# Softmax maxima folded by DMAs through memory, and a division with five transposes in the side bank: one change to an attention and feed-forward kernel on one Trainium2 core

## The chip, the cores and the metric

The kernel runs on one core of one Trainium2 chip. The metric is the device time of one execution in microseconds (us). The engines are named as in the profile: PE is TensorE (PEld its weight loads), DVE is VectorE, ACT is ScalarE, POOL is GpSimd and SP is SyncE, which here issues most DMAs. An engine takes its instructions in order. SBUF is the on-chip memory; PSUM is the memory that PE writes, here eight banks of 128 partitions x 512 fp32.

## The reference

```python
x = x + layernorm(attention(layernorm(x)))          # x: 4 x 1024 x 256, fp32
x = x + layernorm(ffn(layernorm(x)))

# attention, 16 heads of 16
scores = q @ k.T / sqrt(16)
exp_x = exp(clip(scores - max(scores), -50, 50))
attn = exp_x / (sum(exp_x) + 1e-6)
y = (attn @ v) @ Wout.T
# ffn, ternary weights with a scale for each output; hidden size 1024
h = silu(x @ w1.T * s1) * (x @ w2.T * s2)
h = gelu(h @ h1.T * sh1); h = gelu(h @ h2.T * sh2)
y = h @ w3.T * s3
```

The kernel takes the exponential without subtracting the maximum. The sum of the exponentials then has to get eps times the exponential of the maximum in place of eps, so a maximum of each row is wanted once, in the division at the end. (The program takes the maximum over keys only for the first 128 queries of each half; for the others it tests a bound on the scores, and a general version stands behind a branch.)

## The kernel before

**Attention stage.** The work is cut into 32 units: 4 batches (b) x 4 groups of 4 heads (g) x 2 halves of 512 queries (h). Units are numbered 0 to 31 in that order, so an even number is a first half (h = 0) and an odd one a second half. A unit has 16 tiles: 8 chunks of 128 keys x 2 pairs of heads. For a tile, `exponentials` (L444) makes two score products on PE (L451, `s`), into one two-bank PSUM buffer of the pool `ps` (tag "big", three buffers), and one exponential of 128x1024 on ACT (L452, `e`) into a ring of eight tiles in SBUF. For each chunk, `weigh` (L454) multiplies the exponentials of four heads with the values (L459, `acc`, one PSUM bank; the profile shows a chunk as x8); a row of ones among the values gives the sum. For each chunk but the first, `rise` (L461) takes the running maximum over chunks on DVE (L468, `top`, 128 keys x 4 heads x 128 queries).

**Turns.** The order is written out by the loop at L937. A turn makes three tiles (`TURN`), issues the maxima of tiles that earlier turns made, weighs the chunks that are ready (one or two, `a` or `aa` below), and then takes one step of side work that uses PE, with such steps as use no PE. The side work (`Side`, L551) is a list of chains of steps; a step has a gap, the number of turns that it keeps from the step before it in its chain. Chains in `first` go before the others. It holds the next batch's layer norm, transposes (L301), projections (`p`), values (`pv`) and checks (`pn`, `pr`), the output projection of the batch that ends (L506, `py`), and the division of each unit. All but the division use the one PSUM bank `misc` (the side bank). The eighth bank is `acc`.

**A unit's end** (`unit_end`, L632): DVE moves `acc` to SBUF (L265, `o`), and the division (`divide`, L470) is queued as a step with a gap of 1, that is for the side work of the same turn. It takes one of the three "big" buffers: four transposes of `top` into one bank (L478), four of `o` into the other (L480); DVE takes the maximum over the 128 keys from PSUM (L482, `em`), adds eps times it to the sums (L485), copies the others (L486), inverts (L487) and multiplies into `on` (L488). While it holds that buffer, `side.borrowed` makes the next turn begin with two tiles, with the third after its weighing (L940, L959).

**SP's queue.** At the end of a second half, `stack` (L419) issues 32 copies of 64 KB from SBUF to SBUF (L413), which lay out the q and k of the group after the next. Their target is free when the last score product of the unit that just ended has read it. Near the end of the stage SP also issues the loads of the feed-forward weights (L683): twelve after unit 27, four after unit 29.

**Feed-forward stage** (from about 645 us): 8 halves of 512 rows, PE nearly always busy. `prepare` (L707) normalises the next half and transposes it into the side bank (L728), as steps of side work.

Of the kernel before, what the change touches and what calls it, by code (L numbers as in the profile page):

```python
# [25 lines left out]
ROWS = PARTS * DH  # L26
RING = 8
TURN = 3
LN_EPS = 1e-5
# [86 lines left out]
def tile_fast(ctx: ExitStack, tc: tile.TileContext, x, wqk, wv, wo, w1, w1s, w2, w2s, h1, h1s, h2, h2s, w3, w3s, out, bad):  # L116
# [12 lines left out]
    small = ctx.enter_context(tc.tile_pool(name="small", bufs=3))  # L129
    dram = ctx.enter_context(tc.tile_pool(name="rounded", bufs=1, space=bass.MemoryType.DRAM))  # L130


# [45 lines left out]
    with ExitStack() as actx, ExitStack() as rctx:  # L178
# [88 lines left out]
        def prologue(b, space, copy):  # L267
# [61 lines left out]
            def squares(w, m, h):  # L329
                def run():  # L330
                    sq = st["sq", w, m] = work.tile([P, NQ], BF16, tag="sq", name="sq", bufs=4)
                    hi = cq[w, m, "hi"][:, h * NQ : (h + 1) * NQ].bitcast(F32)
                    nc.scalar.activation(sq, hi, AF.Square)

                return run
# [125 lines left out]
        def rise(k):  # L461
# [4 lines left out]
            if c:  # L466
                top = tops[b, g, h]
                nc.vector.tensor_max(top, top if c > 1 else pair(k - 2)[:, :, :, 0:P], pair(k)[:, :, :, 0:P])  # L468

        def divide(g, h, o, top):  # L470


            def run():
                side.borrowed = True
                both = ps.tile([P, 2, NQ], F32, tag="big", name="po")
                po, pm = both[:, 0], both[:, 1].rearrange("p (i k) -> p i k", k=P)
                for i in range(HPG):
                    nc.tensor.transpose(pm[:, i], top[:, i // 2, i % 2], ident)  # L478
                for t in range(TPQ):
                    nc.tensor.transpose(po[:, t * P : (t + 1) * P], o[:, t * P : (t + 1) * P], ident)  # L480
                em = small.tile([P, HPG], F32, tag="em", name="em")
                nc.vector.tensor_reduce(em, pm, AX.X, ALU.max)  # L482
                po = po.rearrange("p (t i s) -> p t i s", t=TPQ, s=SLOT)
                den = small.tile([P, TPQ, HPG], F32, tag="den", name="den")
                nc.vector.scalar_tensor_tensor(den[:, 0], em, SM_EPS, po[:, 0, :, DH], ALU.mult, ALU.add)  # L485
                nc.vector.tensor_copy(den[:, 1:], po[:, 1:, :, DH])  # L486
                nc.vector.reciprocal(den, den)  # L487
                nc.vector.tensor_mul(  # L488
                    on[h][:, :, HPG * DH * g : HPG * DH * (g + 1)].rearrange("p t (i e) -> p t i e", e=DH),
                    po[:, :, :, 0:DH], den.unsqueeze(3).to_broadcast([P, TPQ, HPG, DH]),  # L490
                )

            return [Step(run, 1)]
# [57 lines left out]
        class Side:  # L551


            def __init__(self):
                self.first, self.rest, self.slot = [], [], 0
                self.tired = False
                self.borrowed = False

# [23 lines left out]
            def take(self, calm=False):  # L582

                self.slot += 1
                self.borrowed = False
                free, heavy = True, False
                for chain in self.first + self.rest:
                    while (step := self.due(chain, self.slot, free)) and (step.tensor or not calm):
                        chain[0].pop(0)
                        chain[1] = self.slot  # L590
                        step.run()
                        free = free and not step.tensor
                        heavy = heavy or step.heavy
                self.tired = heavy
# [6 lines left out]
        accs, tops, ends, later = {}, {}, {}, {"qk1": None}  # L601

        def begin(b):

            if b + 1 < B:
                norm, xt, qk, v, flags = prologue(b + 1, misc, to_vector)

                def first_made():
                    later["qk"] = b + 1
                    side.add(flags[0])  # L610

                def second_made():
                    later["qk1"] = b + 1
                    side.add(flags[1])

# [16 lines left out]
        def unit_end(b, g, h):  # L632
# [4 lines left out]
            assert g or not b or not any(step.tensor for step in ends[b - 1, h][0])  # L637
            unit = side.add(divide(g, h, o, tops[b, g, h]), True)
            if g == NG - 1:
# [13 lines left out]
            if at < B:  # L653
                put = Step(slots(at, n), 0, False)
                if at > b:
                    assert later["qk"] == at
                    later["chain"][0].append(put)
                else:
                    assert later["qk1"] == at
                    put.run()  # L660
                stack(at, n)
            if g == NG - 3 and b + 1 < B:
# [44 lines left out]
        def prepare(n, copy):  # L707
# [26 lines left out]

            return norm_steps(rows, st) + [Step(apply(i), 1, False) for i in range(0, TPQ, 2)] + [Step(transposes(c), 1) for c in range(DC)]

# [187 lines left out]
        early = [v[1], Step(slots(0, 0, 0, NT // 2), 0, False)]  # L924
        side.add(early + v[2:] + [Step(slots(0, 0), 0, False), Step(slots(0, 1), 0, False)] + sum(qk[1], []) + [Step(lambda: later.update(qk1=0, v=0), 0, False), Step(lambda: side.add(flags[0] + flags[1]), 0, False)])
        begin(0)
# [10 lines left out]
        while weighed < len(tiles):  # L937
            n = end = made
            end += TURN
            make(end - side.borrowed)  # L940
            if made == len(tiles):
# [262 lines left out]
```

## Time and profile before

| | us |
|---|---|
| median of 3 runs (1323.52 to 1325.0) | 1324.16 |
| the profiled execution, its own time | 1322.63 |
| its span | 1320.8 |
| attention stage, about | 17 to 645 |
| PE busy, share of the span | 1267.2 (96%) |
| ACT busy | 724.1 (55%) |
| DVE busy | 696.2 (53%) |
| POOL busy | 119.1 (9%) |

The shares are means over two stages with different limits: ACT is busy 83 to 89% of each 100 us between 100 and 600 us, and 186 of the 670 us from 650 us on. PE's busy time holds matmuls whose ends are modelled, and matmuls on different rows or columns of the array overlap. In a group's line, the first number after the bar is the busy time, the second the mean duration in ns, and after the second bar stands the engine's idle time just before these instructions, with what ended it.

### The profile page before, as it was taken

What the parts mean: (1) busy time and instruction counts of PE and PEld (TensorE: products, weight loads), DVE (VectorE), ACT (ScalarE), POOL (GpSimd) and SP (SyncE); (2) the same over time, 40 slices, a digit from 0 to 9 for tenths busy, and PEclk for the clock granted to TensorE, in tenths of its full rate; (3) what the DMA queues carried; (4) which work ended last, traced back from release to release, by engine and by line L of the source; (5) the groups of instructions that cost most, each with busy time, mean ns of one, the idle gap of its engine ahead of it and who ended that gap; (6) DMA issues with size and microseconds to landing.
All of it is one profiled execution on the core that took longest, in us unless ns stands there. A gap on an engine that the chain in (4) does not pass through costs nothing.

```text
span 1320.8 us, 21125 instructions
## 1 busy us (share of the span) xinstructions
PE 1267.2 (96%) x8194; PEld 777.2 (59%) x8194; DVE 696.2 (53%) x1518; ACT 724.1 (55%) x902; POOL 119.1 (9%) x166
## 2 busy tenths in 40 slices
PE   7999999999999999988999999999999999999995
PEld 3333333333333333333578888788887888878885
DVE  3456457654685445645662634736446364463533
ACT  4788887888888888898631412314223142231410
POOL 6212112121120000000000000000000000000000
PEclk9999999999999999999999999999999999999998
DMA  4685543466443333343220000201101011020000
GB/s 131 171 212 131 118 114 94 110 143 152 73 114 61 50 50 65 65 95 129 80 113 1 24 1 1 64 25 32 56 1 64 24 33 57 1 64 8 17 0 19
DMA packets 45518, 91.30 MB, mean 69 GB/s; under 512 B 12000, under 2 KB 22880, under 8 KB 45408
## 3 DMA queue, kind: packets, MB, share of 16 engines
q1 hardware_dynamic: 37520, 65.20, 21.4%
q0 software_dynamic: 7360, 24.12, 5.8%
q8 instruction: 67, 1.10, 0.4%
q10 hardware_dynamic: 528, 0.52, 0.1%
q14 instruction: 43, 0.35, 0.1%
HBM read 40.52 MB, written 15.73 MB: 43 GB/s over the span
## 4 chain that ended last, share of the span: by engine, by line
PE 76%; DVE 10%; ACT 9%; issue 3%; POOL 1%; DMA 1%; SPq 0%; ACTq 0%; POOLq 0%; DVEq 0%
PE ph L739 35%; PE acc L459 12%; PE s L451 8%; ACT e L452 7%; PE pg L739 5%; PE pz L792 4%; PE p L259 4%; PE py L259 2%; PE pv L259 2%; DVE top L468 2%; PE po L480 1%; DVE sg L755 1%; DVE o L265 1%; DVE st L94 1%; DVE ha_lo L744 1%
## 5 line engine op out<-in xcount | busy, mean ns | idle before, releaser
L452 ACT ACTIVATE e<-s 128x1024 f32<-128x1024 f32 x512 | 485.1, 1034 | 54.5 <-PE s L451 42.9
L459 PE MATMUL acc<-e,vaug 128*32 128x512 f32 x2048 | 255.1, 600 | 2.6 <-POOL vaug L429 2.6
L775 ACT ACTIVATE a<-ph,h_scale 128x512 f32<-128x512 f32 x128 | 81.1, 686 | 306.6 <-PE ph L739 306.6
L451 PE MATMUL s<-sq,sk 64*128 64x512 f32 x1024 | 193.2, 449 | 17.6 <-ACT e L452 15.0
L739 PE MATMUL ph<-hb_hi,h 128*128 128x512 f32 x512 | 199.5, 390 | 0.0
L739 PE MATMUL ph<-hb_lo,h 128*128 128x512 f32 x512 | 199.4, 389 | 0.0
L451 PEld LDWEIGHTS s<-sq,sk 64*128 64x128 f32 x1024 | 86.2, 184 | 158.3 <-ACT e L452 125.8
L468 DVE TENSOR_TENSOR top<-top,e 128x512 f32<-128x512 f32 x192 | 134.6, 701 | 42.0 <-ACT e L452 35.4
L459 PEld LDWEIGHTS acc<-e,vaug 128*32 128x32 f32 x2048 | 49.2, 108 | 107.2 <-issue 97.6
L104 POOL TENSOR_TENSOR rstd<-ve,minus_half 128x4 f32<-128x4 f32 (+1 forms) x33 | 37.5, 1137 | 803.1 <-DVE ve L102 803.1
L739 PEld LDWEIGHTS ph<-hb_hi,h 128*128 128x128 f32 x512 | 96.1, 188 | 20.2
L739 PEld LDWEIGHTS ph<-hb_lo,h 128*128 128x128 f32 x512 | 96.1, 188 | 20.1
L776 DVE CAST ha_hi<-a 128x512 fp32r<-128x512 f32 x64 | 27.1, 424 | 142.5 <-ACT a L775 142.5
L739 PE MATMUL ph<-ha_hi,sq 128*128 128x512 f32 x256 | 101.8, 398 | 0.3
L739 PE MATMUL ph<-ha_lo,sq 128*128 128x512 f32 x256 | 99.9, 390 | 0.0
L739 PE MATMUL ph<-ha_lo,sk 128*128 128x512 f32 x256 | 99.7, 390 | 0.0
L739 PE MATMUL ph<-ha_hi,sk 128*128 128x512 f32 x256 | 99.7, 390 | 0.0
L753 ACT ACTIVATE sg<-pg,w_scale 128x512 f32<-128x512 f32 x64 | 43.3, 688 | 55.0 <-DVE ha_lo L744 43.1
L755 DVE SCALAR_TENSOR_TENSOR sg<-pg,w_scale,sg 128x512 f32<-128x512 f32 x64 | 47.1, 745 | 48.0 <-ACT sg L753 48.0
L776 DVE CAST hb_hi<-a 128x512 fp32r<-128x512 f32 x64 | 27.0, 422 | 71.3 <-ACT a L775 71.3
L259 PE MATMUL p<-xT,wqk_sb 128*32 128x512 f32 x512 | 61.1, 598 | 1.5 <-ACT xT L262 0.9
L739 PEld LDWEIGHTS ph<-ha_hi,sq 128*128 128x128 f32 x256 | 48.4, 189 | 12.7 <-DVE sg L755 3.3
(158 smaller groups left out, 1648.2 us busy)
## 6 DMA issues: line engine op xcount, KB each, us to landing
w<-in_h_dram POOLq DMA_DIRECT2D x16, 512.0 KB, 5.5
h_r<-wr POOLq DMA_DIRECT2D x16, 512.0 KB, 3.8
x<-in_h_dram SPq DMA_DIRECT2D x32, 256.0 KB, 2.7
sk<-ck1hi SPq DMA_DIRECT2D x64, 64.0 KB, 2.3
sk<-ck1lo SPq DMA_DIRECT2D x64, 64.0 KB, 2.3
sq<-cq1hi SPq DMA_DIRECT2D x64, 64.0 KB, 2.3
sq<-cq1lo SPq DMA_DIRECT2D x64, 64.0 KB, 2.3
h<-h_r SPq DMA_DIRECT2D x8, 512.0 KB, 6.5
```

The source lines that it names most:

```text
L104: nc.gpsimd.tensor_tensor(rstd[:, :n], ve[:, :n], self.minus_half[:, :n], ALU.pow)
L259: nc.tensor.matmul(o[j : j + SLOT, :], w[:, j : j + SLOT], i, **flags)
L451: nc.tensor.matmul(s[:, a, :], stacks[1, g % 2, u][r, c * P : (c + 1) * P], stacks[0, g % 2, u][r, h * NQ : (h + 1) * NQ], start=True, sto ...
L452: nc.scalar.activation(pair(k)[:, u], s, AF.Exp)
L459: nc.tensor.matmul(acc[SLOT * i : SLOT * (i + 1), :], vaug[g % 2][:, c, i, :], pair(k)[:, i // 2, i % 2, :], start=c == 0, stop=c == NT - 1)
L468: nc.vector.tensor_max(top, top if c > 1 else pair(k - 2)[:, :, :, 0:P], pair(k)[:, :, :, 0:P])
L739: nc.tensor.matmul(p, homes[n][c][:, m * P : (m + 1) * P], half[:, c, :], start=c == 0 and k == 0, stop=c == len(homes[n]) - 1 and k == 1)
L753: nc.scalar.activation(sg, p[:, 0, :], AF.Silu, scale=scales["w1"][:, m : m + 1])
L755: nc.vector.scalar_tensor_tensor(sg, p[:, 1, :], scales["w2"][:, m : m + 1], sg, ALU.mult, ALU.mult)
L775: nc.scalar.activation(a, p[:, j, :], AF.Gelu, scale=scales[n][:, m : m + 1])
L776: nc.vector.tensor_copy(o[0][:, m, :], a)
L792: nc.tensor.matmul(p[t], half[:, c, t * P : (t + 1) * P], homes["w3"][c], start=c == 0 and k == 0, stop=c == HC - 1 and k == 1)
```

## The change

The division of 30 of the 32 units is split into transfers, a fold and a shorter division.

- At a unit's end, `divide` at once issues five DMAs on SP: `top` is spilled to a buffer in device memory (256 KB), and for each of the four heads it is read back (64 KB) into `folded`, so that 32 partitions hold one head, and four keys of it lie side by side. Reading back waits for the spill to land; the spill waits for the last maximum. These DMAs stand in SP's queue ahead of the stack copies of the same `unit_end`.
- A step `fold` (no PE; gap 4 in first halves, 3 in second halves) takes two maxima on DVE, over 128x256 and 128x128, which leaves 32 partial maxima for each head.
- A step `run` (gap 1 behind the fold) does four transposes of `o` and one of `folded` into the side bank. The fifth writes into columns of `o`'s slots that are not otherwise used (`HOLE`). DVE's reduction reads 128x(4x32) from there. What follows is as before.
- No turn is shortened: `side.borrowed` is gone.
- The last two units keep the old division (`divide_last`).
- Small moves: the two chains of checks (`flags`) become one; the stack copies may be issued later where the second half of q and k isn't ready (`pending`); the buffer `sq` has two copies instead of four; in `prepare` the first transpose keeps a gap of 2 instead of 1.

```diff
+    shuffle = ctx.enter_context(tc.tile_pool(name="shuffle", bufs=2, space=bass.MemoryType.DRAM))
...
-                    sq = st["sq", w, m] = work.tile([P, NQ], BF16, tag="sq", name="sq", bufs=4)
+                    sq = st["sq", w, m] = work.tile([P, NQ], BF16, tag="sq", name="sq", bufs=2)
...
+        def quotients(g, h, em, po):
+            den = small.tile([P, TPQ, HPG], F32, tag="den", name="den")
+            nc.vector.scalar_tensor_tensor(den[:, 0], em, SM_EPS, po[:, 0, :, DH], ALU.mult, ALU.add)
+            nc.vector.tensor_copy(den[:, 1:], po[:, 1:, :, DH])
+            nc.vector.reciprocal(den, den)
+            nc.vector.tensor_mul(
+                on[h][:, :, HPG * DH * g : HPG * DH * (g + 1)].rearrange("p t (i e) -> p t i e", e=DH),
+                po[:, :, :, 0:DH], den.unsqueeze(3).to_broadcast([P, TPQ, HPG, DH]),
+            )
+
         def divide(g, h, o, top):
+            there = shuffle.tile([P, HPG, P], F32, tag="top", name="top_d")
+            nc.sync.dma_start(out=there, in_=top.rearrange("p u n q -> p (u n) q"))
+            folded = work.tile([P, P // SLOT, P], F32, tag="folded", name="folded", bufs=1)
+            for i in range(HPG):
+                nc.sync.dma_start(out=folded[SLOT * i : SLOT * (i + 1)], in_=there[:, i, :].rearrange("(s k) q -> k s q", k=SLOT))
+
+            def fold():
+                for n in (2, 1):
+                    nc.vector.tensor_max(folded[:, 0:n], folded[:, 0:n], folded[:, n : 2 * n])
+
             def run():
-                side.borrowed = True
+                p = misc("po")
+                for t in range(TPQ):
+                    nc.tensor.transpose(p[:, t * P : (t + 1) * P], o[:, t * P : (t + 1) * P], ident)
+
+                pm = p.rearrange("p (n s) -> p n s", s=SLOT)[:, :, HOLE : HOLE + P // (TPQ * HPG)]
+                nc.tensor.matmul(pm, folded[:, 0], ident.rearrange("p (n k) -> p n k", n=TPQ * HPG), start=True, stop=True, is_transpose=True)
+                em = small.tile([P, HPG], F32, tag="em", name="em")
+                nc.vector.tensor_reduce(em, pm.rearrange("p (i n) k -> p i n k", i=HPG), AX.XY, ALU.max)
+                po = p.rearrange("p (t i s) -> p t i s", t=TPQ, s=SLOT)
+                quotients(g, h, em, po)
+
+            return [Step(fold, 3 if h else 4, False), Step(run, 1)]
+
+        def divide_last(g, h, o, top):
+            def run():
                 both = ps.tile([P, 2, NQ], F32, tag="big", name="po")
...
-                po = po.rearrange("p (t i s) -> p t i s", t=TPQ, s=SLOT)
...
+                quotients(g, h, em, po.rearrange("p (t i s) -> p t i s", t=TPQ, s=SLOT))
...
-            unit = side.add(divide(g, h, o, tops[b, g, h]), True)
+            unit = side.add((divide_last if (b, g) == (B - 1, NG - 1) else divide)(g, h, o, tops[b, g, h]), True)
...
-                    assert later["qk1"] == at
                     put.run()
-                stack(at, n)
+                    if later["qk1"] == at:
+                        stack(at, n)
+                    else:
+                        later["pending"] = lambda: stack(at, n)
...
-            return norm_steps(rows, st) + [Step(apply(i), 1, False) for i in range(0, TPQ, 2)] + [Step(transposes(c), 1) for c in range(DC)]
+            return norm_steps(rows, st) + [Step(apply(i), 1, False) for i in range(0, TPQ, 2)] + [Step(transposes(c), 1 if c else 2) for c in range(DC)]
...
-            make(end - side.borrowed)
+            make(end)
```

## The prediction, made before the changed kernel ran

> **What bounds the kernel now.** I read the page's busy shares first, then five stretches of time, then the groups of 100 to 600 us, then the timelines of PE, ACT, DVE and SP. The attention stage ends at about 645 us, and the feed-forward stage after it hardly changes, so the question is what ends a turn before 645 us. The stretches give ACT 83 to 89% and PE 92 to 97%:
>
> ```profile
> 200.00:300.00 100.00, 94.61 (x808) 35.74 (x800) 63.14 (x135) 82.91 (x97) 21.88 (x28) 1.00 0.48 118
> 400.00:500.00 100.00, 96.60 (x818) 35.35 (x810) 44.10 (x80) 84.64 (x97) 1.80 (x3) 1.00 0.30 49
> ```
>
> The columns are the stretch, its length, the busy time of PE, PEld, DVE, ACT and POOL, the clock, the DMA share and GB/s. The groups of 100 to 600 us say who waits for whom:
>
> ```profile
> L452 ACT ACTIVATE e<-s 128x1024 f32<-128x1024 f32 x418 | 396.0, 1035 | 43.9 <-PE s L451 34.2 <-DVE top L468 6.0 <-ACT e L452 3.2
> L451 PEld LDWEIGHTS s<-sq,sk 64*128 64x128 f32 x834 | 69.7, 184 | 126.8 <-ACT e L452 103.1 <-issue 19.5 <-ACT sq L333 0.3
> ```
>
> The scores wait for ACT to free their banks (103.1 us), so ACT's exponentials set the pace; ACT itself is held 34.2 us by late scores. The stage lasts as long as ACT is busy plus ACT's idle time. A change that adds no ACT work moves the stage by what it does to that idle time. A division turn (PE, then ACT, then DVE):
>
> ```profile
> 555.38 1.92 PE L459 MATMUL acc<-e,vaug 128*32 128x512 f32 x16
> 557.23 0.66 PE L478 MATMUL po<-ident,top 128*128 128x128 f32 x4
> 558.11 0.66 PE L480 MATMUL po<-ident,o 128*128 128x128 f32 x4 [0.23 <-DVE o L265]
> 558.70 0.73 PE L451 MATMUL s<-sq,sk 64*128 64x512 f32 x4
> 559.36 1.06 PE L459 MATMUL acc<-e,vaug 128*32 128x512 f32 x8
> 560.38 0.73 PE L451 MATMUL s<-sq,sk 64*128 64x512 f32 x4
> ...
> 559.30 4.69 ACT L452 ACTIVATE e<-s 128x1024 f32<-128x1024 f32 x5 [1.65 <-PE s L451]
> ...
> 558.81 0.69 DVE L482 TENSOR_REDUCE em<-po 128x4 f32<-128x512 f32 x1 [0.75 <-PE po L480]
> ```
>
> Two weighings and eight transposes stand before the next scores, ACT runs dry for 1.65 us, and the next turn makes two tiles (s x4), not three, ahead of its weighing.
>
> **What goes away.** I cut the timelines into 166 turns of three exponentials (from 44.7 us on) and summed ACT's idle time by turn: 82.6 us. The 31 division turns hold 24.3 of it (16 with one weighing, mean 0.51; 15 with two, mean 1.08). The other 135 hold 58.3, 22.7 of that in the 35 turns whose order a borrowed bank breaks. In the changed order no turn is broken; 9 of the 30 new divisions stand after one weighing and 21 after two. Their price: turns that have four transposes in the side bank today cost 0 to 0.39 us typically after one weighing, 0.5 to 0.82 after two; the fifth adds 0.17 (four take 0.66). I take 0.25 and 0.85: 9 x 0.25 + 21 x 0.85 = 20.1 us. The rest, count in the changed order times today's mean, after one / after two weighings: nothing 13 x 0.00 / 22 x 0.12; projection 24 x 0.38 / 3 x 1.12; values 11 x 0.51 / 1 x 1.2 (estimate); output projection 10 x 0.66 / 3 x 1.13; four transposes 12 x 0.15 / 16 x 0.57; pn 2 x 0.00 / 14 x 0.27; pr 1 x 0.00 / 3 x 0.59; one old division 0.51. Sum 49.0. So 69.1 remain: **13.5 us gained**. With new divisions at 0.1 and 0.6, 20; at today's 0.51 and 1.08, 7. The later first transpose in the feed-forward is worth at most the 2.2 us in all that L728 waited for fxn; I take 0.
>
> DVE loses a 0.69 us reduction and gains one of a quarter of it (about 0.27) and two maxima (0.42 and 0.27, from the 128x256 row of L488): +0.27 us a unit on an engine that is 44 to 63% busy, beside ACT: nothing, while that cover holds. Transfers grow by 512 KB a unit, at a DMA share of 0.3 to 0.5: nothing by themselves.
>
> **What is added: a wait on SP, and one on DVE.** Each unit's five DMAs go through SP's queue: the spill waits for the last maximum, the four reads wait for the spill to land, the DVE fold waits for the reads. I call the end of the unit's last maximum R. The nearest rows: output stores of 128 and 384 KB land in 1.7 and 2.8 us, so the 256 KB spill in 2.3; copies of 64 KB land in 2.3:
>
> ```profile
> sk<-ck1hi SPq DMA_DIRECT2D x64, 64.0 KB, 2.3
> out_dram<-z SPq DMA_DIRECT2D x7, 384.0 KB, 2.8
> out_dram<-z SPq DMA_DIRECT2D x11, 128.0 KB, 1.7
> ```
>
> Issues take 0.33 to 0.59 us. Chain: 2.3 + 3 x 0.5 + 2.3 = 6.1 us (1 less to 3 more: these rows include landings of 4 to 6 us when much is in flight).
>
> Second halves: SP is free at R, data at R + 6.1. The order puts two or three maxima of the next unit before the fold, which stood at R + 6.0 to 13.1 in this trace. Hidden. But the 32 stack copies queue behind that chain. They now start 3 to 8 us ahead of R (SP waited 211.8 us for scores, L413), and will start at R + 4.3, some 9 us later; they land 10 to 17 us before use, less two shorter units: 1 to 4 us are left, and under 1 before units 28 and 30. I take 0.5 us.
>
> First halves: R falls in the middle of those copies. A block takes 20.7 to 23.8 us, so SP is free at R(second) + 26, and a unit takes 15.8 to 20.9. The spill waits 4.4 to 9.6 us, data come at R + 10.5 to 15.7, the fold stands at R + 10.3 to 15.3. Unit by unit from this trace's times DVE would stand still 1.9 us (unit 2), 2.3 (4), 3.4 (6), 4.1 (10), 3.1 (14), 2.0 (18), 1.1 (22), 4.3 (26), others under 1; 0.8 more each as units get shorter. Behind it on DVE stand maxima (L468), lo parts (L325) and copies out of the side bank (L265), for which PE's next side work waits. PE comes to that work 4.1 us (median) after DVE's last maximum, so 2.6 us of stall are hidden where a copy out stands behind the fold, and 3.9 where only the maxima's transpose waits. What shows: 0.1, 0, 0.3, 2.3, 0, 0.2, 0, 1.2: 4 us. One us more on every chain makes it 10, two 18, one less 1.5. I take 6 for the early units, whose transfers meet loads.
>
> Unit 28 (batch 3, group 2, first half) stands apart. Between the copies and its spill, SP issues twelve weight loads that wait for each other:
>
> ```profile
> 569.15 1.14 SPq L413 DMA_DIRECT2D sk<-ck1hi  x2
> ...
> 590.36 0.53 SPq L683 DMA_DIRECT2D ck0hi<-w_r  x1
> ...
> 592.49 1.87 SPq L683 DMA_DIRECT2D ck1hi<-w_r  x4
> 594.47 4.95 SPq L683 DMA_DIRECT2D ck1lo<-w_r  x4
> ```
>
> That is 9.1 us after 21.1 of copies. Unit 27's last maximum ends at 573.3; copies start at 577.7, loads end at 607, unit 28's chain at 613.4, the fold 0.8 later. PE reaches that division near 604. **About 10 us** are lost (7 to 13), with nothing behind which to hide: PE stands, and ACT runs dry.
>
> The Trainium skill ("DMA: Bandwidth & Descriptors", Anatomy of one DMA) speaks against this change: a DMA costs about 2 us however small, mostly the receipt of the last byte, with an especially long delay when the target is HBM, and a semaphore wait is served on the issuing sequencer, not by the DMA engine. Its fit of 2.0 us plus bytes over 436e3 (for DMAs from GpSimd) makes the chain 2.6 + 1.5 + 2.15 = 6.25 us where the rows give 6.1; the total would rise by 1 us.
>
> **Sum.** -13.5 + 0.5 + 6 + 10 = +3.0 us. The profiled execution took 1322.6 us (span 1320.8), so 1325.6; the median shown is 1324.16, 1.5 above it: **1327 us**. About 0.2% (2.6 us) is what a measurement can tell from no change.
>
> **Rivals.**
> 1. *The cover holds (faster).* The chain lands a us sooner, or DVE reaches the fold later than in this trace, and only unit 28 pays, 7 us: -16 + 7 + 1 = -8, about 1316; if the loads don't hold SP either, 1310. For: eight stalls lie within 1.6 us of being hidden. Against: the order of SP's queue is fixed, and its 26 us are measured. 30%.
> 2. *The round trip is longer (slower).* Reading back what was just written costs 1.5 to 2 us more than the rows of 64 KB. Stalls 14 to 18, unit 28 12, late stacks 2: 1339 to 1343. It decides from about 7 us per chain on. For: loads in this trace land in up to 6 us. Against: from 400 us on the queues are half empty. 20%.
> 3. *The side bank takes the third bank's place*, so that the change doesn't do what it says: the DVE chain from em to on takes 1.7 us, and the next side work stands 1.9 us of PE behind it. If DVE is late by 1 us, ten to fifteen turns lose it, and the gain is 3: 1333. 5%.
>
> The forecast has 45%, its own range is 1321 to 1333; 17% of it lies within 0.2%, 28% above. Faster: 30 + 2 (of rival 3) = 32%. Slower: 28 + 20 + 3 = 51%. The range takes in rival 1 beyond its 1316 and rival 2 up to its middle: 1312 to 1341, with some 2 in 10 left out.
>
> **What would show it.** ACT's idle time between 45 and 645 us: 69 us without the stalls, some 85 with them. L452 held by PE s less often in ordinary turns. DVE waiting for DMA folded at units 6, 10, 14 and 26 for 2 to 5 us, and at unit 28 for over 10 us; PE po waiting there too. SP's sk copies starting after R. I am wrong if the wait at unit 28 is short (SP or the loads were quicker), or if first halves wait over 6 us each.

## The result, and the profile after

The changed kernel takes **1362.37 us** (median, 1357.45 to 1370.42, 4 runs) against 1323.84 before (1322.67 to 1325.0): ratio 1.0297, 95% interval 1.0246 to 1.0348. It is 38.5 us slower. The forecast was 1327.0 with a range of 1312 to 1341: the sign was the likelier one, the size is outside the range. The profiled execution took 1362.28 us with a span of 1360.5. Lines of the changed kernel are those of its own file: L454 is the exponential, L453 the scores, L461 the weighing, L487 the spill, L490 the reads, L494 the fold, L499 and L502 the transposes of `o` and of `folded`.

The stretches that were shown of before, of the changed kernel (columns: the stretch, its length, busy time of PE, PEld, DVE, ACT, POOL, granted clock, DMA share, GB/s):

```profile
200.00:300.00 100.00, 86.77 (x711) 32.98 (x707) 61.27 (x143) 77.82 (x90) 17.33 (x23) 0.95 0.48 119
400.00:500.00 100.00, 93.31 (x829) 35.95 (x821) 62.25 (x146) 87.31 (x102) 9.82 (x12) 1.00 0.45 102
```

PE and ACT both lost 5 to 8 us in the first hundred and PE's granted clock is below 1 there. From 400 to 500 us ACT gained (84.64 to 87.31). By then the two kernels are not at the same work at the same time, so this is only a hint that the change saves in some places and waits in others; kernel 4 below tells the two apart. The groups of 44 to 686 us tell what it waits for:

```profile
L454 ACT ACTIVATE e<-s 128x1024 f32<-128x1024 f32 x501 | 473.9, 1037 | 86.3 <-PE s L453 77.5 <-DVE top L470 4.2 <-ACT e L454 3.6
...
L494 DVE TENSOR_TENSOR folded<-folded 128x256 f32<-128x256 f32 (+1 forms) x60 | 22.2, 370 | 96.6 <-DMA folded<-top_d 91.7 <-DMA sk<-ck0hi 3.1 <-issue 0.7
```

DVE stood still for 91.7 us until what was read back had landed, in 15 waits, one in each of the 15 first halves that have the new division. From its first to its last exponential ACT was busy 527.0 us and idle 87.6 before, and is busy 526.1 and idle 131.4 now. The part of the span outside of that fell from 706.2 to 703.0.

**Where the transfers land.** The transfers themselves are as quick as the prediction's rows had them:

```profile
top_d<-top SPq DMA_DIRECT2D x30, 256.0 KB, 2.4
folded<-top_d SPq DMA_DIRECT2D x120, 64.0 KB, 2.0
```

From the start of the spill's issue to the last read's landing, 24 of the 30 chains take 5.3 to 7.4 us (median of all 5.9; predicted 6.1), six take 8.0 to 13.7 while other transfers are in flight. The estimate from the Trainium skill's fit ("DMA: Bandwidth & Descriptors", Anatomy of one DMA), 6.25 us, is near that median; but the fit is for DMAs from GpSimd, and from there the chains of kernel 1 below took 6.7 to 13.3 us, median 8.1. What is late is the start. Unit 28, timelines of SP, DVE, PE and ACT (start, length, then what):

```profile
628.63 2.49 SPq L415 DMA_DIRECT2D sq<-cq1lo  x4
631.22 0.53 SPq L724 DMA_DIRECT2D ck0hi<-w_r  x1
...
636.28 3.87 SPq L724 DMA_DIRECT2D ck1lo<-w_r  x4
640.26 0.36 SPq L487 DMA_DIRECT2D top_d<-top  x1
643.29 1.74 SPq L490 DMA_DIRECT2D folded<-top_d  x4
```

```profile
646.74 0.75 DVE L494 TENSOR_TENSOR folded<-folded 128x256 f32<-128x256 f32 x2 [16.64 <-DMA folded<-top_d]
```

```profile
633.59 0.66 PE L499 MATMUL po<-ident,o 128*128 128x128 f32 x4
647.54 0.47 PE L502 MATMUL po<-ident,folded 128*128 128x128 f32 x1 [13.29 <-DVE folded L494]
```

```profile
648.81 2.85 ACT L454 ACTIVATE e<-s 128x1024 f32<-128x1024 f32 x3 [13.65 <-PE s L453]
```

The last maximum of unit 28 ended at 620.8. SP was still issuing stack copies, then twelve weight loads, and came to the spill 19.5 us later. DVE waited 16.64 us, PE 13.29 of them, ACT 13.65: the wait is handed on from queue to queue. This is the step that the prediction worked out (10 us, 7 to 13).

Unit 0 is one that it did not work out. SP's timeline there:

```profile
62.33 8.64 SPq L198 DMA_DIRECT2D wo_sb<-in_wo_dram  x16
71.01 3.91 SPq L148 DMA_DIRECT2D x<-in_x_dram  x8
...
77.49 0.43 SPq L208 DMA_DIRECT2D w3s_sb<-in_w3s_dram  x1
78.68 0.33 SPq L487 DMA_DIRECT2D top_d<-top  x1
81.27 1.76 SPq L490 DMA_DIRECT2D folded<-top_d  x4
```

Unit 0's last maximum ended at 54.5; SP had the loads of the start before it until 78. DVE waited 18.7 us, and ACT 17.9, its longest gap between exponentials (timelines of DVE and ACT):

```profile
84.76 0.75 DVE L494 TENSOR_TENSOR folded<-folded 128x256 f32<-128x256 f32 x2 [18.75 <-DMA folded<-top_d]
88.34 1.94 ACT L454 ACTIVATE e<-s 128x1024 f32<-128x1024 f32 x2 [17.90 <-PE s L453]
```

### The profile page after: what moved, and what is told of

It is laid out like the page before. It is cut to its first block, busy times and chain, and to the rows that moved or that the text cites. A ratio compares the mean times of both kernels' runs of the same rounds, so it can differ in the third digit from the quotient of the medians.

```text
span 1360.5 us, 21239 instructions
## 1 busy us (share of the span) xinstructions
PE 1258.5 (93%) x8104; PEld 773.2 (57%) x8104; DVE 699.6 (51%) x1578; ACT 722.9 (53%) x902; POOL 117.3 (9%) x166
## 4 chain that ended last, share of the span: by engine, by line
PE 68%; DVE 9%; DMA 7%; SPq 7%; ACT 6%; issue 2%; ACTq 0%; POOL 0%; DVEq 0%; POOLq 0%
PE ph L780 34%; PE acc L461 10%; PE s L453 7%; SPq L415 4%; ACT e L454 4%; PE pz L833 4%; PE pg L780 3%; PE p L261 3%; DMA folded<-top_d 2%; PE py L261 2%; DVE sg L796 2%; DMA top_d<-top 2%; PE pv L261 2%; SPq L490 1%; DVE ha_lo L785 1%
## 5 line engine op out<-in xcount | busy, mean ns | idle before, releaser
L454 ACT ACTIVATE e<-s 128x1024 f32<-128x1024 f32 x512 | 484.4, 1036 | 87.6 <-PE s L453 78.8
L461 PE MATMUL acc<-e,vaug 128*32 128x512 f32 x2048 | 263.6, 618 | 1.0 <-POOL vaug L431 1.0
L453 PE MATMUL s<-sq,sk 64*128 64x512 f32 x1024 | 188.1, 452 | 18.1 <-ACT e L454 14.7
L453 PEld LDWEIGHTS s<-sq,sk 64*128 64x128 f32 x1024 | 87.4, 189 | 138.5 <-ACT e L454 108.3
L461 PEld LDWEIGHTS acc<-e,vaug 128*32 128x32 f32 x2048 | 50.1, 110 | 111.1 <-issue 106.3
L105 POOL TENSOR_TENSOR rstd<-ve,minus_half 128x4 f32<-128x4 f32 (+1 forms) x33 | 37.6, 1138 | 818.1 <-DVE ve L103 818.1
L494 DVE TENSOR_TENSOR folded<-folded 128x256 f32<-128x256 f32 (+1 forms) x60 | 22.2, 370 | 96.6 <-DMA folded<-top_d 91.7
```

Of the source, the lines that this page charges most:

```text
L453: nc.tensor.matmul(s[:, a, :], stacks[1, g % 2, u][r, c * P : (c + 1) * P], stacks[0, g % 2, u][r, h * NQ : (h + 1) * NQ], start=True, sto ...
L454: nc.scalar.activation(pair(k)[:, u], s, AF.Exp)
L461: nc.tensor.matmul(acc[SLOT * i : SLOT * (i + 1), :], vaug[g % 2][:, c, i, :], pair(k)[:, i // 2, i % 2, :], start=c == 0, stop=c == NT - 1)
```

## The experiments

Every kernel was timed beside the kernel before on the same chip; the kernel before had medians of 1322.8 to 1324.1 there, and kernels of different groups are compared by their ratios to it. Theory A is the prediction's mechanism: the place in SP's queue makes the transfers late, and DVE and PE wait behind the fold. Its rivals are that the transfers themselves are slow (B), and that the side bank or the new order costs (C).

**1. All five transfers on another queue.**

```diff
-            nc.sync.dma_start(out=there, in_=top.rearrange("p u n q -> p (u n) q"))
+            nc.gpsimd.dma_start(out=there, in_=top.rearrange("p u n q -> p (u n) q"))
...
-                nc.sync.dma_start(out=folded[SLOT * i : SLOT * (i + 1)], ...)
+                nc.gpsimd.dma_start(out=folded[SLOT * i : SLOT * (i + 1)], ...)
```

> The five transfers of a division are issued by GpSimd instead of SyncE; nothing else changes. Theory A (the loss is the place in SyncE's queue: in first halves the spill waits there behind the stack copies, in unit 0 behind the first loads, in unit 28 behind the weight loads, and DVE, the side bank and PE wait for the fold): the spill goes out within a few us of the last maximum, the fold waits for DMA fall from 92 us in all to under 25, and the time from 1362 to 1312 to 1322. Rival B (the round trip through memory is itself too slow for the fold's place, whatever queue issues it): second halves stay as they are, first halves wait on, 1345 or more. Rival C (the side bank and the five transposes cost, and the fold's wait only shows it): 1350 to 1360.

Measured: **1305.92 us**, ratio 0.9871 (0.9837 to 0.9905): 56 us quicker than the changed kernel, and faster than the kernel before. The same transfers, fold and division are there; only the queue differs. The chains even take longer there (median 8.1 us from the start of the spill's issue, where SP's took 5.9), but all spills go out 0.3 us after the last maximum. DVE's wait fell to a quarter (44 to 630 us):

```profile
L494 DVE TENSOR_TENSOR folded<-folded 128x256 f32<-128x256 f32 (+1 forms) x60 | 22.9, 382 | 24.5 <-DMA folded<-top_d 23.5
```

Theory A holds for most of the loss; B and C cannot explain it.

**2. The copies on two queues**, the transfers staying on SP.

```diff
-                for copy in copies(g, w):
-                    copy(nc.sync)
+                for n, copy in enumerate(copies(g, w)):
+                    copy((nc.sync, nc.gpsimd)[n % 2])
```

> Every second stack copy is issued by GpSimd, so that SyncE has 16 copies behind a second half's transfers instead of 32 and is free some 11 us earlier. Theory A: the spills of first halves wait 0 to 2 us instead of 4 to 12; the ACT gaps at units 2, 8, 12 and 26 (26 us) go, the one at unit 28 falls from 13.7 to about 4, the one at unit 0 (17.9) stays, since no copies stand before it: about 1324. Rival B: the data are as late from the spill on, at most 10 us go: 1350 or more. If GpSimd issues its copies late, PE waits for stacks instead, which would show as scores waiting for sk or sq.

Measured: 1339.34, ratio 1.0133 (1.0116 to 1.015). Better than the change, but 15 us worse than expected. 10.7 us of it are lost at the start, because the same fault came up in the other queue: GpSimd's half of the copies stood ahead of its copy of the values, and the first weighing waited for that. Later some chains took up to 13.5 us, and folds of second halves waited too (3.6 us in unit 5, 5.9 in unit 13), which had been no part of theory A.

```profile
43.09 0.48 POOL L415 DMA_DIRECT2D sq<-cq0lo  x1 [0.43 <-DMA sk<-ck0lo]
...
43.57 0.41 POOL L431 COPY vaug<-cv 128x256 f32<-128x256 f32 x1
...
44.03 1.94 PE L461 MATMUL acc<-e,vaug 128*32 128x512 f32 x8 [12.28 <-POOL vaug L431]
```

**3. The old division at units 0 and 28** of the changed kernel: `(b, g, h) in ((0, 0, 0), (B - 1, NG - 2, 0))` is added to the condition for `divide_last`.

> Units 0 and 28 keep the old division, the other 28 the new one. Theory A: the two longest gaps of ACT (17.9 and 13.7 us) go, and the two units give back about 1 us: 1362 - 31 = 1331. Rival D (the waits are spread over all units, and the clock's fall after them carries the loss; these two gaps only move elsewhere): 1345 or more.

Measured: 1333.85, ratio 1.0075 (1.0058 to 1.0092): 28.5 us of the loss sat at these two units, net of what moved: unit 1, whose spill goes out 5.2 us late behind the same first loads and whose chain then takes 11.4 us, now waits (a gap of 8.7 us in ACT at 84 us).

**4. No transfers.** The fold takes the unit's maxima directly, over heads instead of over keys, so another maximum enters the division; all else stays.

```diff
-            there = shuffle.tile([P, HPG, P], F32, tag="top", name="top_d")
-            nc.sync.dma_start(out=there, ...)
...
-            for i in range(HPG):
-                nc.sync.dma_start(out=folded[SLOT * i : SLOT * (i + 1)], ...)
...
-                for n in (2, 1):
-                    nc.vector.tensor_max(folded[:, 0:n], folded[:, 0:n], folded[:, n : 2 * n])
+                both = top.rearrange("p u n q -> p (u n) q")
+                nc.vector.tensor_max(folded[:, 0:2], both[:, 0:2], both[:, 2:4])
+                nc.vector.tensor_max(folded[:, 0:1], folded[:, 0:1], folded[:, 1:2])
```

> The spill and the reads are left out; the fold takes its maxima straight from top, over the four heads instead of over keys, so that the maximum that is used is another one, and all instructions of PE, DVE and ACT and their order are those of the changed kernel. Theory A: no division turn waits, and what is left is the gain that was forecast, 13.5 us: 1308 to 1313. Rival C (side bank instead of third bank): PE waits for DVE between the division and the next side work, 1318 to 1326.

Measured: **1290.93**, ratio 0.9758 (0.9741 to 0.9774). So the gain side is 32 us, not the prediction's 13.5, and the loss side is 71 us, not 16.5. Both terms were too small, and in the sum the two errors partly cancel: that its sign came out right is in part luck. ACT's idle time is 61.1 us here. Laid over this kernel unit by unit, the changed kernel is longer by 17.5 us where unit 0's division falls, by 14.4 around unit 28's, and by 40 in the units between, mostly at units 2 (3.8), 4 (4.6), 8 (7.2), 10 (3.8), 12 (8.7), 16 (1.8), 20 (2.0) and 26 (3.9).

**5. Transfers kept, and nobody waits for them.** Kernel 4 with the five transfers back in SP's queue, read into a buffer `unread` (in device memory, where the changed kernel reads into SBUF, so the traffic is not quite the same).

```diff
+            there = shuffle.tile([P, HPG, P], F32, tag="top", name="top_d")
+            nc.sync.dma_start(out=there, in_=top.rearrange("p u n q -> p (u n) q"))
+            unread = shuffle.tile([P, P // SLOT, P], F32, tag="unread", name="unread")
+            for i in range(HPG):
+                nc.sync.dma_start(out=unread[SLOT * i : SLOT * (i + 1)], ...)
```

> The five transfers of each unit are issued from SP's queue as in the changed kernel, but what is read back lies in another buffer that nobody reads, and the two maxima of the fold take the unit's maxima directly, over heads, as in the kernel without transfers (so another maximum enters the division). Theory A (place in SP's queue: what costs is that DVE, and PE behind it, wait for the data): with nobody waiting the time is that of the kernel without transfers, 1290.9, plus late stack copies of 1 to 5 us: 1291 to 1296. Rival B (the traffic itself, or the stack copies that stand behind it in SP's queue): 1305 or more, ACT idle above 75 us instead of 61.

Measured: 1303.64, ratio 0.9842 (0.9825 to 0.9858). The total lies near B's bound, but the place speaks for A: 8.2 us more lie in the stretch of unit 2's exponentials and 5.4 in that of unit 4, and from unit 6 on no unit differs from kernel 4 by more than 0.9 us, most by under 0.02. Unit 4's loss is stack copies that start 22 us after unit 1's last maximum, behind the first loads and the transfers (10 us in kernel 4). Unit 2's is a wait that the prediction did not have: `top` has two buffers, and unit 2's first maximum must wait until unit 0's spill has left its buffer.

```profile
84.23 0.89 DVE L470 TENSOR_TENSOR top<-e,e 128x512 f32<-128x512 f32 x1 [7.93 <-DMA top_d<-top]
```

So after the start neither the traffic nor the stack copies that start some 9 us later cost anything by themselves.

**6. Shortened turns again**, in kernel 4 (`side.borrowed` set in `run`, and `make(end - side.borrowed)`).

> The kernel without transfers, in which the turn after each division makes two tiles ahead of its weighing instead of three, as before the change. Theory O (the gain is the unbroken order of the turns): 15 to 25 of the 32 us go again, 1306 to 1316. Rival S (the gain is the division's place in the side bank and its fewer transposes): 1291 to 1298.

Measured: 1296.42, ratio 0.9795 (0.9778 to 0.9811). The unbroken order is worth some 5 us (5.5 by the medians, 4.9 by the ratios). The prediction had put the greater part of its 13.5 there; rival S is right.

**7. The old division everywhere, with the rest of the change** (`divide_last` at every unit, with its shortened turns).

> The changed kernel with the old division at every unit (eight transposes in the third bank, shortened turns, no transfers): what is left of the change is one chain for the bounds, two buffers for sq instead of four, the later put of stacks, and the gap of two turns ahead of the first transpose of each feed-forward half. If the 3.4 us that the kernel without transfers gained outside the exponentials come from that gap, 1319 to 1320 with the attention stage unchanged; if they come from the division, 1322 to 1324. Should the chain and sq be worth something in the attention stage too, below 1318.

Measured: 1318.14, ratio 0.996 (0.9946 to 0.9974). The rest of the change gains 5 us by itself, about half of it outside the exponentials (703.7 us against 706.3); 22 of the 32 us come from the division's form (kernel 7 to kernel 6).

**8. GpSimd's queue, and the old division at units 0, 1 and 28.**

> The five transfers issued by GpSimd, and the old division at units 0, 1 and 28, where the transfers still ran into loads of weights. The kernel with GpSimd's queue took 1305.9 and idled some 13 us at units 0, 1, 26 and 28 that the kernel without transfers did not; three old divisions cost about 3 us. Theory A: 1297 to 1301, faster than all kernels whose output is the reference's. If it stays above 1304 the waits only move on to the next units, as the 8.7 us at unit 1 did when the old division stood at units 0 and 28 alone.

Measured: 1299.71, ratio 0.9825 (0.9809 to 0.9842), as A had it.

**9. The first loads elsewhere**: output weights, two batches of x and scales are issued by GpSimd, one piece at each of the first five unit ends.

```diff
+            if b == 0:
+                load_rest(NH * g + h)
             if h < NH - 1:
                 return
```

> The changed kernel with the loads of the output projection, of two batches of x and of the scales (some 18 us of SP's queue, up to 79 us) issued by GpSimd in pieces, one at each of the first five unit ends. Theory A (unit 0's division is late because its spill stands behind these loads in SP's queue): the 17.9 us of ACT idle in unit 1's window fall under 2, unit 2's and 4's (4.7 and 2.8) by about half, total 1338 to 1345. Rival B (the transfers themselves are slow while the weights are loaded): 1355 or more, the wait stays at 10 us or more.

Measured: 1349.83, ratio 1.0208 (1.0191 to 1.0225). Unit 0's wait is gone, as A says, but only 12.5 of the expected 17 to 24 us come back: without it units 1 and 2 come sooner, unit 1's copies still hold SP, and unit 2's spill is issued 13.7 us after its last maximum (at 89.7). ACT's gap there is 10.5 us.

```profile
99.63 2.48 SPq L416 DMA_DIRECT2D sq<-cq1lo  x4
103.40 0.35 SPq L488 DMA_DIRECT2D top_d<-top  x1
```

**10. The weight loads elsewhere** (`load_weights` issues on GpSimd instead of SP).

> The changed kernel with the loads of the feed-forward weights issued by GpSimd instead of SP. Theory A (unit 28's chain stands behind twelve of them in SP's queue): the 13.7 us wait of unit 28 falls under 3, total 1348 to 1353. Rival B (the loads' traffic delays the chain whoever issues them, as the spill of 6.9 us with GpSimd's queue hints): 6 to 8 us stay, total 1356 to 1359.

Measured: 1359.43, ratio 1.0273 (1.0246 to 1.0301); unit 28 still waits.

```profile
625.92 2.48 SPq L415 DMA_DIRECT2D sq<-cq1lo  x4
628.50 0.53 SPq L487 DMA_DIRECT2D top_d<-top  x1
633.18 1.73 SPq L490 DMA_DIRECT2D folded<-top_d  x4
```

The interval overlaps that of the changed kernel, so the edit's effect on the time is not told apart from none. My expectation of under 3 us was wrong, in the first place by theory A itself: ahead of the spill stand the stack copies too, which end at 628.4, 10.6 us after unit 28's last maximum. But rival B has a share here. The spill starts 8.9 us earlier than in the changed kernel, and the last read lands only 4.8 us earlier, because the chain takes 10.4 us beside the loads (6.4 in the changed kernel). ACT's loss at this unit falls from 14.4 to 12.2 us only.

**11. First halves by GpSimd, second halves by SP**, old division at units 0, 1 and 28 (`queue = nc.sync if h else nc.gpsimd`).

> As the kernel with GpSimd's queue and old divisions at units 0, 1 and 28 (1299.7), but the transfers of second halves go through SP again, which is free then; the stack copies start behind them. The late copies cost nothing from unit 6 on in the kernel whose transfers nobody reads. The waits of 0.4 to 2.7 us of the second halves' folds vanish: 1296 to 1299. If the copies come late for first halves of the next group, 1301 or more.

Measured: **1294.7** (1291.38 to 1295.28), ratio 0.9784 (0.9768 to 0.9801): 28.5 us faster than the kernel before, the fastest of the kernels that leave nothing out. Each queue now gets the transfers at a time when it is free; DVE's wait for data is 0.2 us (44 to 630 us):

```profile
L495 DVE TENSOR_TENSOR folded<-folded 128x256 f32<-128x256 f32 (+1 forms) x54 | 19.1, 354 | 4.0 <-DMA sk<-ck0hi 2.9 <-DMA folded<-top_d 0.2
```

**12. Kernel 8 with the fold of second halves one turn later**, save in a batch's last group.

> As the kernel with GpSimd's queue and old divisions at units 0, 1 and 28 (1299.7), with the fold of second halves four turns behind the unit's end instead of three, except in the last group of a batch. The waits of second halves' folds vanish, the division goes one turn on: 1297 to 1300; if the later division collides with other side work, 1301 to 1304.

Measured: 1298.53, ratio 0.9809 (0.9793 to 0.9825). The interval overlaps that of kernel 8: the edit's effect is not told apart from none. Kernel 11, on the same chip, is quicker: its highest time, 1295.28, is below this kernel's lowest, 1297.36.

**13. First halves by GpSimd alone** (no old division but in the last two units).

> The changed kernel with the transfers of first halves alone issued by GpSimd; second halves stay in SP's queue, and every unit but the last two has the new division. Theory A (place of first halves in SP's queue, behind stack copies and loads): the waits of units 0 to 28 fall to what GpSimd's queue leaves (13 us at units 0, 1, 26 and 28 with all transfers there), 1299 to 1306. If second halves in SP's queue cost too, by late stack copies, 1308 or more.

Measured: 1301.23, ratio 0.9834 (0.9819 to 0.9849). Moving the transfers of first halves alone brings 61 of the 71 us back. 7.9 us of the rest lie in one place, where unit 1's fold waits 8.4 us; its spill, still on SP, is issued 5.1 us after its last maximum, behind the first loads. No other unit loses over 2.2 us, and unit 28 loses 0.4.

**14 and 15. The later first transpose in the feed-forward**, alone on the kernel before, and taken back in kernel 4.

```diff
-            return norm_steps(rows, st) + [...] + [Step(transposes(c), 1) for c in range(DC)]
+            return norm_steps(rows, st) + [...] + [Step(transposes(c), 1 if c else 2) for c in range(DC)]
```

> The kernel before with one edit: the first transpose of each feed-forward half one turn later. Theory F (the some 3 us gained outside the exponentials come from this): span less the exponentials falls by 2.5 to 3.5 us, total 1319.5 to 1321. Rival (they come from the end of the attention stage): 1322.5 to 1324.

> The kernel without transfers (1290.9) with the first transpose of each feed-forward half one turn after the norm, as before the change. Theory F: 1293.5 to 1294.5. Rival: 1290.5 to 1291.5.

Measured: 1319.45, ratio 0.9969 (0.9957 to 0.9981), and 1295.78, ratio 0.9785 (0.977 to 0.98) against kernel 4's 0.9758: the edit is worth about 4 us either way (theory F). The groups of 640 to 1320 us, first of the kernel before, then of kernel 14:

```profile
L728 PE MATMUL fpt<-ident,fxn 128*128 128x128 f32 x56 | 11.8, 291 | 0.0
...
L728 PEld LDWEIGHTS fpt<-ident,fxn 128*128 128x128 f32 x56 | 7.3, 139 | 5.4 <-DVE fxn L112 2.2 <-issue 1.3
```

```profile
L728 PE MATMUL fpt<-ident,fxn 128*128 128x128 f32 x56 | 8.4, 272 | 0.0
...
L728 PEld LDWEIGHTS fpt<-ident,fxn 128*128 128x128 f32 x56 | 6.9, 140 | 1.9
```

Not only the 2.2 us named DVE went: the weight loads' whole idle time fell by 3.5 us, and the transposes' busy time by 3.4.

**16. Four more transposes** in each division of kernel 4 (those of `o` made twice).

```diff
-                for t in range(TPQ):
+                for t in [*range(TPQ), *range(TPQ)]:
```

> The kernel without transfers (1290.9) with the four transposes of o made twice in each of the 30 new divisions: 120 matmuls more on PE, 0.5 us of PE's busy time a unit by what the old division's four more took (37.6 less 22.6 us over 30 units), 0.66 by the group of four alone. Theory P (PE, busy 545.5 of 570 us there, sets the pace of the attention stage): +13 to +20 us, 1304 to 1311. Theory of the prediction (ACT sets the pace, and four more transposes cost only the difference between a turn's classes, 0.2 to 0.5 us in 21 divisions and less in 9): +4 to +9 us, 1295 to 1300.

Measured: 1301.69, ratio 0.9832 (0.9813 to 0.9851), 10.8 us more than kernel 4 by the medians (9.8 by the ratios). That is between the two expectations. In the trace the transposes of the divisions took 12.9 us more of PE's busy time (0.43 a unit, less than I had assumed), and from 44 us to the last exponential the kernel is 10.5 us longer. 1.7 of these are not the transposes' own: at 551.8 us PE is granted half its clock for 3.41 us, which kernel 4 has nowhere in this stretch. What is left, 8.8 us, is two thirds of PE's added time. So PE's work counts for the greater part here, which the prediction's classes did not have; but neither theory fits alone.

**17. Kernel 13 with unit 1's transfers on GpSimd as well** (`queue = nc.sync if h and (b, g) != (0, 0) else nc.gpsimd`).

> As the kernel with the first halves' transfers alone issued by GpSimd (1301.2), with unit 1's five transfers there too. Theory A (unit 1's spill stands behind the first loads in SP's queue): most of the 7.9 us go, 1294 to 1297. If unit 1's reads are slow for the traffic of the first loads (both of these units' chains took 6 to 8 us of GpSimd's queue in the kernel with all transfers there, with 4.3 and 2.4 us of ACT idle), 1298 to 1300.

Measured: 1300.2, ratio 0.9817 (0.9801 to 0.9834). The second expectation is the right one, and theory A fails at this unit: the spill is now issued 0.3 us after the last maximum, but it lands 6.9 us later and the last read 13.3 us after the maximum, while the first loads are in flight; the fold still waits 7.7 us and the unit loses 6.2. So B is right where much is in flight, at the start, and wrong for the 12 chains of the changed kernel from unit 18 on, of which none takes over 7.0 us.

## Why the prediction was wrong, step by step

The mechanism of the loss was right: the place in SP's queue makes the transfers late, and the wait is handed on to PE and ACT. Three steps failed. Unit 0 was put among the "others under 1" and cost 17.5 us. "I take 6" for the other first halves came out as 40 us: DVE stood still for 56 us where 22 to 32 were forecast, and PE's clock, which fell after long waits, was no term of the sum at all. And the gain of 13.5 us, priced by ACT's idle time in turns of the old order, was 28 in the attention stage.

| step | predicted | measured | from |
|---|---|---|---|
| gain in the attention stage | -13.5 | -28 | kernel 15 against before |
| feed-forward | 0 | -4 | kernels 14, 15 |
| late stack copies | +0.5 | 0 after unit 4 | kernel 5 |
| unit 0 | none | +17.5 | after against kernel 4 |
| first halves 2 to 26 | +6 | +40 | same |
| unit 28 | +10 | +14 | same |

**The gain: the price of PE's work.** The prediction let ACT set the pace and priced a turn by ACT's idle time. These two stretches, first of the kernel before, then of kernel 4, say what it left out:

```profile
44.00:642.00 598.00, 567.54 (x4672) 212.07 (x4664) 337.81 (x707) 514.54 (x585) 75.95 (x99) 1.00 0.46 104
```

```profile
44.00:614.00 570.00, 545.47 (x4594) 204.00 (x4586) 341.32 (x767) 513.77 (x587) 75.72 (x100) 1.00 0.48 109
```

ACT is busy as long as before, PE 22 us less, and the stretch is 28 us shorter. (By ACT's idle time it is the same: 82.6 us fall to 55.1 in the prediction's 166 turns, where it had 69.1.) PE was busy 95% of it before the change, with 30 us idle in all; ACT had 83 idle. The scores that "wait for ACT" for 103.1 us on PEld are weight loads held back while other matmuls run; the matmuls themselves stood idle for ACT for only 15.0 us, and that in the longer stretch of 44 to 642 us:

```profile
L451 PE MATMUL s<-sq,sk 64*128 64x512 f32 x1000 | 188.7, 450 | 16.4 <-ACT e L452 15.0
```

The divisions' transposes took 37.6 us of PE's busy time before and 22.6 in kernel 4: 15.0 us, where the prediction's classes gave the division turns 4.2. The shortened turns took 5.3 us of PE's busy time (550.5 against 545.2 in kernels 6 and 4, from 44 us to the last exponential). The price of a new division after one weighing, 0.25 us, was exact; after two it was 0.58, not 0.85; and the classes whose order did not change got cheaper too (values 0.51 to 0.30, output projection 0.66 to 0.45), which class means from the old order could not show. Of the 14.0 us between 69.1 and 55.1, 5.7 lie in the 21 new divisions after two weighings, the rest in the other classes. That PE's shorter work is the cause is supported by kernel 16, two thirds of whose added PE time came out as time, and not shown for every class. How the rest of the 22 us of kernel 7 to 6, some 4 us of PE idle time, divides among the third bank and the DVE chain was not tried.

**Unit 0: one queue read too short.** The prediction counted only the copies in front of the first halves' spills and said "others under 1". SP's timeline of the kernel before had the first loads in it; they end at 78 us in the changed kernel, 24 us after unit 0's last maximum. Kernels 3 and 9 show it.

**The first halves: the stalls twice too small, and a term that was not there.** The spill starts 4.0 to 11.8 us after the last maximum (predicted 4.4 to 9.6), because the copies, which begin 3.9 to 5.5 us after a second half's last maximum, end 3.9 to 11.7 us after the next one. With R for the end of the unit's last maximum, the data are there at R + 10.8 to 18.7 (predicted 10.5 to 15.7), also because four of these chains take 8.0 to 13.7 us. And DVE comes to the fold at R + 8.1 to 12.8, where the prediction had 10.3 to 15.3. So DVE stands still for 56 us in units 2 to 26 (predicted 22, and 10 more with the 0.8 a unit for shorter units); units 8, 12 and 20, which were to lose nothing, stood for 6.1, 10.6 and 5.1 us.

The cover held on the whole: in this part of the kernel PE is idle 25.9 us longer than in kernel 4, so 30 of the 56 us were hidden, 2.3 in each of the 13 units, where the prediction took 2.6 or 3.9. The other 14.1 of the 40 us are PE being busy longer with the same work. PE's missing clock there (busy time times the share of the clock that was not granted) is 14.7 us; the last section has the lines. The prediction's sum had no term for this. That the cover is a mean can be seen at unit 8, where a check's reduction stands right behind the fold, and PE waits for it 5.71 us:

```profile
246.40 0.75 DVE L494 TENSOR_TENSOR folded<-folded 128x256 f32<-128x256 f32 x2 [6.11 <-DMA folded<-top_d]
247.07 0.67 DVE L359 TENSOR_REDUCE norm<-pn 64x4 f32<-64x512 f32 x1
```

```profile
247.80 3.64 PE L261 MATMUL py<-wo_sb,oT 128*32 128x256 f32 x32 [5.71 <-DVE norm L359]
```

**Unit 28** was sized at 10 us and took 14: SP reached the spill 19.5 us after the last maximum, held by the loads and copies that the prediction had named. The data came at R + 25.9, where the prediction's times give 23.6, and PE is busy 1.3 us longer there than in kernel 4.

**Rivals.** Rival 2 (a longer round trip) had the nearest total, 1339 to 1343, for a reason that among the changed kernel's first halves holds only at units 6, 12, 14 and 16: the median chain is 5.9 us. Rival 3 is out: the division's new form is the greater part of the gain. (Its total was also added up wrongly: with a gain of 3 in place of 13.5 the prediction's own terms give some 1337, not 1333.) Rival 1's mechanism did not occur.

**What would have shown it.** ACT's idle time was to be 69 us without stalls and some 85 with them; by the same turns it is 55 (kernel 4) and 126. "I am wrong if first halves wait over 6 us each" has come true for units 0, 8, 10, 12, 26 and 28; the other first halves waited 0.8 to 5.6 us.

## What to carry to other kernels

A DMA that must start soon goes to a queue whose earlier entries have been listed one by one at that time: here the same five transfers cost 71 us on SP's queue behind copies and loads, and some 10 when first halves go by GpSimd. An engine that is busy 95% of a stage has a price of its own, also where another engine seems to set the pace: here each us more on PE cost about two thirds of a us. And a forecast of long waits of PE needs a term for the clock after them, beside the wait itself.

## What the runs showed of the hardware that was not expected

A long wait of PE costs twice. In the changed kernel from 44 us to the last exponential PE is idle 54.8 us longer than in kernel 4 and busy 16.6 us longer, with the same work. Stretches around unit 8's wait (the clock is the third number from the end):

```profile
236.00:242.10 6.10, 6.09 (x62) 2.04 (x50) 3.92 (x9) 5.15 (x7) 1.21 (x2) 1.00 0.70 189
242.10:247.80 5.70, 0.00 (x1) 0.00 (x1) 1.37 (x4) 1.35 (x2) 0.54 (x1) 0.71 0.43 138
247.80:250.80 3.00, 3.00 (x31) 1.36 (x32) 2.44 (x4) 0.00 (x0) 0.00 (x0) 0.50 0.00 0
251.00:257.00 6.00, 6.00 (x51) 2.36 (x49) 1.97 (x7) 5.00 (x6) 0.13 (x1) 0.97 0.00 0
```

After the wait PE is busy without a break and granted half its clock (the output projection above took 3.64 us for its 32 matmuls; the one at 555 us of the same trace 1.91), and ACT gets no scores in those 3 us. The same follows nine of the thirteen waits of PE over 1.2 us, for 3.2 to 3.5 us in seven of them; summed over PE's busy time the missing clock is 18.7 us, and 0.0 before and in kernel 4. That the clock is the whole of the 16.6 us is argued from this sum, not shown by a run of its own.

In all kept traces together, from 44 us to the last exponential, every half-clock stretch lasts 3.41 us or a multiple of it. One follows each of the 34 waits of PE of 3.0 us or more, 7 of the 10 of 2.0 to 2.5 us, and 3 of the 56 of 1.2 to 2.0 us. Five more follow no wait over 1.1 us: at 596.1 us of the changed kernel the longest wait before was 0.42 us, and PE had been idle for 1.18 of the 3.4 us before. So the single wait does not decide alone; what does is not shown.

The Trainium skill ("TensorE: Matmul & The Clock Gate", Part 1) says that the clock falls to half after an idle window of about 3.4 us and comes back after as long a busy one. The time to come back agrees, but here waits of 1.6, 1.8 and 2.1 us were enough in three cases of the changed kernel, and others of 1.3 to 1.8 us were not followed by it.
